# The spread of dt by DMA in a Mamba layer, begun three groups ahead of its scan instead of two

## The chip, the cores and the metric

The kernel runs on one core of a Trainium2 chip. The metric is the device time of one execution in microseconds, taken as the median of several executions. The engines are named as in the profile: PE is the matrix engine (PEld its loading of weights), DVE the vector engine, ACT the scalar engine with its function tables, POOL the GpSimd engine, and SP the engine whose sequencer, SPq, only issues transfers here.

## The reference, cut to what matters

Four layers follow each other on an image of 2 x 128 x 64 x 64 in float32. The change lies in the first of them, two Mamba blocks over sequences of 4096 tokens, each followed by a feed-forward block:

```python
xz = x @ in_w.T;  u, z = split(xz)
u = silu(causal_conv4(u) + conv_b)
dt, Bm, Cm = split(u @ xproj_w.T)             # 8, 16 and 16 wide
dt = softplus(dt @ dt_w.T + dt_b)             # 256 channels
dA = exp(dt[..., None] * A)                   # 256 channels x 16 states
dBu = (dt * u)[..., None] * Bm[:, :, None, :]
h = dA_t * h + dBu_t                          # for each token in turn
y = sum over states of h * C_t
y = (y + u * D) * silu(z) @ out_w.T
```

The three other layers (two self-attentions over 4096 positions and a multi-scale fusion) are not touched.

## The kernel before, in words

The first layer fills the time from about 60 us to 2190 us. Its work is cut into 32 items, one for each of two images, two blocks and eight chunks of 512 tokens. 256 channels times 16 states are 4096 recurrences, and 128 of them fit on the partitions at once, so an item has 32 scans of 128 x 512. Four scans (m = 0 to 3) share one pack of 32 channels and make a group: the 128 partitions hold the same 32 channels four times over, each time for another state. An item thus has 8 groups; below, "group 6" is the seventh group of an item and "slot 24" its first scan, out of slots 0 to 31.

What a group needs, with the names of the code:

- `dtb`, dt of the 32 channels laid four times over the partitions. `spread_dt(g)` (L325 to L329) does this by four transfers of 64 KB from the tile `dt`, on the SP queue. There are four buffers of it.
- `pdu`, dt times u spread in the same way, but by one matmul (`spread_dtu`, L334) into a PSUM buffer of which there is one. `times_b` (L340, DVE) multiplies it with `bb` into `h`, a tile of four 512-wide parts; five buffers serve `h`, and the hidden tile of the feed-forward block takes turns in them.
- `da`, the exponential of `dtb` times A (`decay`, L347, ACT), four PSUM buffers.
- the scan itself (L358, DVE). After the fourth scan of a group POOL saves the last column (L360) and multiplies `h` by `cb` (L361).
- `y_pair` (L373, PE), sixteen small matmuls that sum two groups over the states; `y_out` (L381, DVE) adds u times D once for each half of an item.

`bb` and `cb` are B and C of an item spread over the partitions. `spread_bc` (L297 to L305) does it once for each item: the tile `dbl`, which the projection `pd` (L291, PE) and a copy on ACT (L295) make, goes to DRAM as `dr`, and from there eight broadcast transfers of 256 KB each bring it back, four for `bb` and four for `cb`. These nine transfers are on the SP queue too.

The order of everything is written out by hand. A main loop goes over items and, within each, over 32 slots: in every slot it emits the spreads that are due, `y_pair`, one scan, the decay of four slots later, `times_b` of the next group, and then the background work of that slot from a list (`background`, L437 to L475): for the next item the convolution matmuls (L262), `xproj` (L291) in slot 13, `spread_bc` in slot 14, `soft_plus` (L315) in slot 17, `dt_end` (L321) in slot 18; for two layer normalisations at once the variance (L210) in slot 17, a Newton step in slots 20 and 21 (L226 on POOL, L227 on ACT, L231 on POOL), its spread over the partitions (`pr`, L235, PE) in slot 27; and the feed-forward block (L403, L415). Each engine runs its own instructions strictly in that order, and so does the queue of SP. An SP instruction whose data or buffer is not ready holds back all transfers behind it. The program also uses eight completion counters in turn for its transfers, so each transfer waits for the one issued eight before it.

Of the kernel before, what the change touches and what calls it, by code (L numbers as in the profile page):

```python
# [6 lines left out]
F32 = mybir.dt.float32  # L7
# [8 lines left out]
P = 128  # L16
CH = 512
# [50 lines left out]
def tile_conv_seq(ctx: ExitStack, tc, x, consts, vecs, wemb, wlay, wconv, wdt, wqkv, wsmall, wms, out):  # L68
# [39 lines left out]
    with ExitStack() as s, tc.manual_schedule():  # L108
        wp = s.enter_context(tc.tile_pool(name="l0w", bufs=1))
        sp = s.enter_context(tc.tile_pool(name="l0s", bufs=1))  # L110
# [23 lines left out]
        for l in range(NL):  # L134
            w = wp.tile([P, NWL - DI], F32, name=f"wl{l}")
# [30 lines left out]
        st = [{} for _ in items]  # L166
# [6 lines left out]
        def vl(name, i, k=0):  # L173
            return v1(f"{name}{items[i][1]}", k)
# [22 lines left out]

        def ln_square(w, k, i):
            if "sq" not in w:
                w["sq"] = sp.tile([P, 2, CH], F32, name="sq", tag="tmp", bufs=2)  # L200
                w["cen"] = sp.tile([P, 2, CH], F32, name="cen", tag="cen")
            pc = w.pop(("pc", k))
            nc.scalar.activation(w["sq"][:, k, :], pc, AF.Square)
            nc.scalar.copy(w["cen"][:, k, :], pc)
# [35 lines left out]

        def ln_shift(w, k, i, second):
            if second:
                dst = st[i]["x2"] = sp.tile([P, CH], F32, name="x2", tag="tmp", bufs=2)
            else:
                xn = st[i]["xn"] = sp.tile([P, KC - 1 + CH], F32, name="xn", tag="xn", bufs=2)
                if items[i][2] == 0:
                    nc.gpsimd.memset(xn[:, : KC - 1], 0.0)
                else:
                    nc.gpsimd.tensor_copy(xn[:, : KC - 1], prev_xn[0][:, CH : CH + KC - 1])
                prev_xn[0] = xn  # L250
                dst = xn[:, KC - 1 :]
            nc.scalar.activation(dst, w["cen"][:, k, :], AF.Identity, bias=vl("ln_b", i))  # L252
# [71 lines left out]
        def spread_dt(g):  # L324
            i, s_ = divmod(g, NST)  # L325
            o = st[i]["dtb", s_] = sp.tile([P, CH], F32, name="dtb", tag="dtb", bufs=4)
            k = 32 * (s_ % 4)
            for q in range(4):
                nc.sync.dma_start(o[32 * q : 32 * q + 32, :], st[i]["dt"][k : k + 32, s_ // 4, :])  # L329

        def spread_dtu(g):
            i, s_ = divmod(g, NST)
            pdu = st[i]["pdu", s_] = bc.tile([P, CH], F32, name="pdu", tag="bc")
            nc.tensor.matmul(pdu, lhsT=four(s_ % 4), rhs=st[i]["dtu"][:, s_ // 4, :], start=True, stop=True)  # L334

        def times_b(g):
            i, s_ = divmod(g, NST)
            h = st[i]["h", s_] = sp.tile([P, 4, CH], F32, name="h", tag="h", bufs=5)
            pdu = st[i].pop(("pdu", s_))
            nc.vector.tensor_tensor(h, st[i]["bc", 0], pdu.unsqueeze(1).to_broadcast([P, 4, CH]), ALU.mult)  # L340

        def decay(t):
            g, m = divmod(t, 4)
            i, s_ = divmod(g, NST)
            j, gg = divmod(s_, 4)
            da = st[i]["da", s_, m] = dap.tile([P, CH], F32, name="da", tag="da")
            nc.scalar.activation(da, st[i]["dtb", s_], AF.Exp, scale=am[items[i][1]][:, j, gg, m : m + 1])  # L347

        def scan(t):
            g, m = divmod(t, 4)  # L350
            i, s_ = divmod(g, NST)
            j, gg = divmod(s_, 4)
            b, l, c = items[i]
            if (b, l) not in carries:
                carries[b, l] = sp.tile([P, NJ, 4, 4], F32, name="carry", tag="carry", bufs=2)
                nc.gpsimd.memset(carries[b, l], 0.0)
            h, da = st[i]["h", s_], st[i].pop(("da", s_, m))
            nc.vector.tensor_tensor_scan(h[:, m, :], da, h[:, m, :], carries[b, l][:, j, gg, m : m + 1], ALU.mult, ALU.add)  # L358
            if m == 3:
                nc.gpsimd.tensor_copy(carries[b, l][:, j, gg, :].unsqueeze(2), h[:, :, CH - 1 : CH])  # L360
                nc.gpsimd.tensor_tensor(h, h, st[i]["bc", 1], ALU.mult)  # L361

        def y_pair(g):

            i, s_ = divmod(g, NST)
            j, gg = divmod(s_, 4)
            if gg == 0:
                st[i]["py", j] = yp.tile([P, CH], F32, name="py", tag="y")
            py = st[i]["py", j]
            for m in range(4):  # L370
                for k in range(2):
                    r = 32 * (gg + k)
                    nc.tensor.matmul(  # L373
                        py[r : r + 32, :], lhsT=sel, rhs=st[i]["h", s_ + k][:, m, :], start=(m == 0), stop=(m == 3),
                        tile_position=(0, r),
                    )
# [60 lines left out]
        def background(i):  # L437
# [28 lines left out]
            for k, (it, second) in enumerate(pair):  # L466
                at(12 + 2 * k, ln_centre, w, k, it)
                at(13 + 2 * k, ln_square, w, k, it)
                at(27, ln_spread, w, k, m), at(28, ln_scale, w, k, it)
                at(29, ln_shift, w, k, it, second)  # L470
# [13 lines left out]
        NG, NT = NI * NST, NI * NSL  # L484
        for i in range(-2, NI + 2):
            todo = background(i)
            for t_ in range(NSL):
                t = i * NSL + t_
                g, m = divmod(t, 4)
                if m == 0 and 0 <= g + 2 < NG:  # L490
                    spread_dt(g + 2)
                if m == 0 and 0 <= g + 1 < NG:
                    spread_dtu(g + 1)
                if m == 0 and g % 2 == 1 and 0 <= g - 3 < NG:
                    y_pair(g - 3)
                if 0 <= t < NT:
                    scan(t)
                if 0 <= t + 4 < NT:
                    decay(t + 4)
                if m == 3 and 0 <= g + 1 < NG:  # L500
                    times_b(g + 1)
                for f, a in todo[t_]:
                    f(*a)
# [14 lines left out]
    with ExitStack() as s, tc.manual_schedule():  # L518
        sp = s.enter_context(tc.tile_pool(name="ats", bufs=1))
# [9 lines left out]
        st = {}  # L529
# [158 lines left out]
        for now in range(NALL + LAG + 10):  # L688
            r, u = divmod(now, NU)
            w = now % 8  # L690
# [31 lines left out]
    with ExitStack() as s, tc.manual_schedule():  # L722
        sp = s.enter_context(tc.tile_pool(name="mss", bufs=1))
# [50 lines left out]
        for si in (2, 3):  # L774
            wgt[si] = sp.tile([P, SCALES[si]], F32, name=f"wgt{si}")
            for k in range(SCALES[si]):
                w = (k + 0.5) / SCALES[si] - 0.5
# [6 lines left out]
        st = [{} for _ in items]  # L784
# [386 lines left out]
```

## Time and profile before

| what | value |
|---|---|
| device time, median of 3 | 5351.36 us (5349.31 to 5352.06) |
| span of the profiled execution | 5360.6 us |
| busy over the span: PE, DVE, ACT, POOL | 91%, 71%, 43%, 43% |
| busy from 60 to 2250 us: PE, DVE, ACT, POOL | 1907.1, 1884.3, 1499.6, 1440.5 us of 2190 |
| granted PE clock from 60 to 2250 us, and after | 0.89 and 0.98 |
| mean time from one item to the next (items 1 to 30) | 65.19 us |
| `dtb` transfers | 1024 of 64 KB, median 2.0 us to landing |
| `bb`, `cb` transfers | 128 each of 256 KB, median 4.5 and 7.6 us to landing |

A group of the profile is all instructions of one line, engine and operation; its line gives the busy time and the mean of one, and after the bar how long the engine stood idle just before them, and what ended that. A wait is always put down to the event that came last. Lines of SPq are issues of transfers, and "to landing" is the time from the start of an issue to the transfer's completion.

### The profile page before, as it was taken

How to read it: one execution, taken by the hardware profiler on the slowest of the kernel's cores; microseconds unless marked ns; L12 is line 12 of the kernel's file. 1: busy time of each engine (PE TensorE's matmuls, PEld its weight loads, DVE VectorE, ACT ScalarE, POOL GpSimd, SP SyncE). 2: the span in 40 equal slices, each digit the busy share in tenths (PEclk: the TensorE clock that was granted, in tenths of full speed). 3: DMA queues.
4: the chain of work that ended last, by engine and by line, in shares of the span. 5: the costliest groups of instructions: out<-in, count | busy, mean ns of one | idle time of the engine just before them, and what ended most of it. 6: DMA issues, size and time to landing. Idle time of an engine off the chain costs nothing.

```text
span 5360.6 us, 48695 instructions
## 1 busy us (share of the span) xinstructions
PE 4900.6 (91%) x15085; PEld 2311.3 (43%) x15085; DVE 3798.2 (71%) x3810; ACT 2326.4 (43%) x2933; POOL 2287.5 (43%) x1948
## 2 busy tenths in 40 slices
PE   5888888888888898899999999999999998988997
PEld 1222222222222222356665566656666665333332
DVE  4998999889999999136663366667767775656665
ACT  4676777777777776212221122232323221223332
POOL 2766666666666767112221122223333332322221
PEclk8898889999898988899999999999999999999998
DMA  4222233222222232014442244444444442000000
GB/s 108 69 65 64 65 70 70 68 68 64 64 64 64 68 73 69 17 42 95 96 97 50 51 96 96 95 101 112 112 101 101 112 111 71 4 4 4 6 6 8
DMA packets 233843, 362.04 MB, mean 68 GB/s; under 512 B 87648, under 2 KB 88048, under 8 KB 225136
## 3 DMA queue, kind: packets, MB, share of 16 engines
q1 hardware_dynamic: 184432, 291.76, 23.2%
q10 hardware_dynamic: 49152, 67.17, 5.2%
q8 instruction: 121, 1.98, 0.2%
q14 instruction: 138, 1.13, 0.1%
HBM read 83.92 MB, written 6.29 MB: 17 GB/s over the span
## 4 chain that ended last, share of the span: by engine, by line
PE 59%; DVE 14%; DMA 10%; ACT 6%; SPq 4%; issue 4%; POOL 4%; ACTq 0%; DVEq 0%; POOLq 0%
PE pq L600 11%; PE po L647 11%; PE py L373 5%; PE pp L544 5%; DVE tr L627 4%; PE pu L262 4%; SPq L638 3%; DMA dtb<-dt 3%; DVE h L358 3%; DMA bb<-dr 3%; POOL h L361 3%; DMA pt<-tr 3%; PE pdu L334 2%; PE pf L861 2%; PE ph L403 2%
## 5 line engine op out<-in xcount | busy, mean ns | idle before, releaser
L634 POOL COPY pt<-tr 32x512 f32<-32x512 f32 x1024 | 628.0, 613 | 1680.7 <-DVE tr L627 911.8
L358 DVE TENSOR_TENSOR_SCAN h<-da,carry,h 128x512 f32<-128x512 f32 x1024 | 1240.2, 1267 | 97.6 <-ACT da L347 68.3
L361 POOL TENSOR_TENSOR h<-h,cb 128x2048 f32<-128x2048 f32 x256 | 1160.7, 4534 | 20.8 <-POOL carry L360 0.2
L604 DVE TENSOR_SCALAR_CACHE_REDUCE sc<-pq 128x1024 f32<-128x1024 f32 x512 | 625.9, 1223 | 760.6 <-PE pq L600 748.4
L647 PE MATMUL po<-pt,vt 128*128 128x256 f32 x4096 | 968.1, 380 | 4.8 <-DMA pt<-tr 4.8
L600 PE MATMUL pq<-k,q 128*128 128x512 f32 x2048 | 962.1, 592 | 4.8 <-ACT q L532 3.4
L647 PEld LDWEIGHTS po<-pt,vt 128*128 128x128 f32 x4096 | 776.4, 190 | 265.4 <-issue 170.6
L347 ACT ACTIVATE da<-dtb,am 128x512 f32<-128x512 f32 x1024 | 686.8, 685 | 390.3 <-DVE h L358 250.2
L613 ACT ACTIVATE sc<-sc,nm 128x4096 f32<-128x4096 f32 x128 | 474.8, 3709 | 721.9 <-DVE nm L611 615.6
L627 DVE STREAM_TRANSPOSE tr<-sc 128x2048 f32<-128x2048 f32 x256 | 589.3, 2302 | 37.9 <-DMA pt<-tr 24.5
L340 DVE TENSOR_TENSOR h<-bb,pdu 128x2048 f32<-128x2048 f32 x256 | 580.0, 2266 | 25.0 <-POOL carry L360 15.4
L373 PE MATMUL py<-h,sel 128*32 128x512 f32 x2048 | 506.7, 638 | 1.7 <-POOL h L361 1.7
L600 PEld LDWEIGHTS pq<-k,q 128*128 128x128 f32 x2048 | 383.5, 190 | 277.8 <-issue 248.7
L334 PE MATMUL pdu<-dtu,fsel 128*128 128x512 f32 x512 | 327.4, 726 | 87.8 <-DVE h L340 87.6
L532 ACT ACTIVATE q<-pqq,vec 128x256 f32<-128x256 f32 x64 | 30.4, 474 | 606.6 <-PE pqq L544 361.2
L373 PEld LDWEIGHTS py<-h,sel 128*32 128x32 f32 x2048 | 114.5, 117 | 412.5 <-issue 406.8
L544 PE MATMUL pp<-xt,wq 128*128 128x512 f32 x576 | 251.8, 598 | 6.6 <-DMA wq<-in_wqkv 6.2
L262 PE MATMUL pu<-xn,wu 128*128 128x512 f32 x512 | 246.1, 614 | 2.7 <-ACT xn L252 1.7
L235 PE MATMUL pr<-rs,kc 2*128 2x512 f32 (+1 forms) x128 | 117.1, 1059 | 133.1 <-POOL rs L231 126.9
L334 PEld LDWEIGHTS pdu<-dtu,fsel 128*128 128x128 f32 x512 | 95.2, 214 | 303.5 <-DVE h L340 187.9
L888 PE MATMUL pqkv<-f,ws 128*128 128x512 f32 x384 | 197.8, 641 | 10.2 <-ACT q L895 6.3
L950 DVE TENSOR_TENSOR ov<-v,pw 128x2048 f32<-128x2048 f32 x64 | 146.2, 2284 | 63.4 <-PE pw L943 63.3
(191 smaller groups left out, 5089.1 us busy)
## 6 DMA issues: line engine op xcount, KB each, us to landing
pt<-tr SPq DMA_DIRECT2D x2048, 64.0 KB, 2.0
dtb<-dt SPq DMA_DIRECT2D x1024, 64.0 KB, 2.0
pt<-tr ACTq DMA_DIRECT2D x1024, 64.0 KB, 2.1
bb<-dr SPq DMA_DIRECT2D x128, 256.0 KB, 4.5
cb<-dr SPq DMA_DIRECT2D x128, 256.0 KB, 7.6
xt<-in_x SPq DMA_DIRECT2D x16, 256.0 KB, 5.1
xr<-in_x SPq DMA_DIRECT2D x16, 256.0 KB, 3.1
out<-ot SPq DMA_DIRECT2D x16, 256.0 KB, 2.0
```

What stands on the lines that cost most here:

```text
L334: nc.tensor.matmul(pdu, lhsT=four(s_ % 4), rhs=st[i]["dtu"][:, s_ // 4, :], start=True, stop=True)
L340: nc.vector.tensor_tensor(h, st[i]["bc", 0], pdu.unsqueeze(1).to_broadcast([P, 4, CH]), ALU.mult)
L347: nc.scalar.activation(da, st[i]["dtb", s_], AF.Exp, scale=am[items[i][1]][:, j, gg, m : m + 1])
L358: nc.vector.tensor_tensor_scan(h[:, m, :], da, h[:, m, :], carries[b, l][:, j, gg, m : m + 1], ALU.mult, ALU.add)
L361: nc.gpsimd.tensor_tensor(h, h, st[i]["bc", 1], ALU.mult)
L373: nc.tensor.matmul(py[r : r + 32, :], lhsT=sel, rhs=st[i]["h", s_ + k][:, m, :], start=(m == 0), stop=(m == 3), tile_position=(0, r),)
L544: nc.tensor.matmul(ps, lhsT=wq[:, which, tap, :], rhs=rhs, start=(tap == 0), stop=(tap == 8))
L600: nc.tensor.matmul(pq[:, i, :], lhsT=st["q", r, grp][:, it * P : (it + 1) * P], rhs=st["k"][:, at : at + CH], start=True, stop=True)
L604: nc.vector.tensor_scalar(dst, pq, 1.0, None, ALU.mult, ALU.max, accum_out=st["mx"][:, c2 : c2 + 1])
L627: nc.vector.transpose(tr, half.rearrange("p (t r f) -> p r t f", r=NB, f=32))
L634: nc.gpsimd.tensor_copy(dst, src)
L647: nc.tensor.matmul(st["po", r, grp], lhsT=st["vt"][:, jt, :], rhs=rhs, start=(jt == 0), stop=(jt == N // P - 1))
```

## The change

`spread_dt` is called three groups ahead of the scan instead of two. The number of `dtb` buffers stays at four. Beside this, two tiles of the layer normalisation, `sq` and `x2`, which shared two buffers, get one of their own each. The purpose is to have the spread dt on hand earlier than the exponentials ask for it.

```diff
         def ln_square(w, k, i):
             if "sq" not in w:
-                w["sq"] = sp.tile([P, 2, CH], F32, name="sq", tag="tmp", bufs=2)
+                w["sq"] = sp.tile([P, 2, CH], F32, name="sq", tag="sq")
...
             if second:
-                dst = st[i]["x2"] = sp.tile([P, CH], F32, name="x2", tag="tmp", bufs=2)
+                dst = st[i]["x2"] = sp.tile([P, CH], F32, name="x2", tag="x2")
...
                 g, m = divmod(t, 4)
-                if m == 0 and 0 <= g + 2 < NG:
-                    spread_dt(g + 2)
+                if m == 0 and 0 <= g + 3 < NG:
+                    spread_dt(g + 3)
                 if m == 0 and 0 <= g + 1 < NG:
                     spread_dtu(g + 1)
```

In the emitted program this moves the four transfers of `dtb` for group 6 of every item from just behind the item's nine transfers `dr`, `bb` and `cb` to just ahead of them; the order of all other transfers of that queue relative to these stays, but for the small loads `xr`, which now stand behind one more group of `dtb`. The order on PE, DVE, ACT and POOL is the same as before.

## The prediction

> **What bounds the kernel now.** I read the waits of DVE first, because in the first layer PE (1907 of 2190 us) and DVE (1884 us) are both nearly full and DVE carries the scans. From 60 to 2250 us, who DVE waited for:
>
> ```profile
> DVE u L381 <- PE py L373: 84.9, 51, 8.6
> DVE h L358 <- ACT da L347: 68.3, 40, 3.8
> ```
>
> The scans waited 68.3 us for an exponential, in 40 places. The same view of ACT and of the SP queue:
>
> ```profile
> ACT da L347 <- DVE h L358: 250.2, 216, 2.9
> ACT da L347 <- DMA dtb<-dt: 133.9, 31, 6.1
> ```
> ```profile
> SPq L300 <- ACT dbl L295: 767.0, 32, 38.2
> SPq L329 <- ACT da L347: 374.2, 95, 9.2
> ...
> SPq L329 <- DMA cb<-dr: 93.3, 128, 2.1
> SPq L329 <- DMA bb<-dr: 56.6, 90, 1.3
> ```
>
> ACT waits for a spread `dtb` once in each item, 4.3 us on average. SPq waits 24 us per item (767.0/32) for `dbl` before it can issue `dr`, and afterwards 128 `dtb` issues, four in each item, wait for the landing of a `cb`: that is the wait for the transfer eight before. So I went through one item by the timeline, item 14. The queue:
>
> ```profile
> 1026.60 0.31 SPq L300 DMA_DIRECT2D dr<-dbl  x1
> 1028.25 1.70 SPq L305 DMA_DIRECT2D bb<-dr  x4
> 1030.05 1.76 SPq L305 DMA_DIRECT2D cb<-dr  x4
> 1031.85 30.59 SPq L329 DMA_DIRECT2D dtb<-dt  x28
> ```
>
> The last `dtb` before this `dr` was issued at 1001.3 us, and then the queue stood for 24.7 us. The first four `dtb` behind `cb` are group 6. Read in narrow windows, the first lands 8.5 us after its issue at 1031.85, the fourth 5.9 us after 1035.22, at 1041.2; an undisturbed one takes 2.0. ACT and DVE at that time:
>
> ```profile
> 1037.50 0.63 ACT L221 ACTIVATE nt<-rs 2x512 f32<-2x512 f32 x1
> 1041.28 0.69 ACT L347 ACTIVATE da<-dtb,am 128x512 f32<-128x512 f32 x1 [3.14 <-DMA dtb<-dt]
> 1041.90 0.70 ACT L227 ACTIVATE nt<-nt,c 2x512 f32<-2x512 f32 x1
> ```
> ```profile
> 1039.66 0.74 DVE L381 SCALAR_TENSOR_TENSOR u<-u,vec,py 128x512 f32<-128x512 f32 x1
> 1042.00 4.85 DVE L358 TENSOR_TENSOR_SCAN h<-da,carry,h 128x512 f32<-128x512 f32 x4 [1.59 <-ACT da L347]
> ```
>
> The scan of slot 24 could have begun at 1040.41 and begins at 1042.00, straight after its exponential. Is this on the path that sets the end? The chain of waits around it:
>
> ```profile
> 1029.53 5.67 DMA bb<-dr
> 1035.20 0.02 issue
> 1035.22 5.95 DMA dtb<-dt
> ...
> 1041.28 0.70 ACT da L347
> 1041.97 0.03 issue
> 1042.00 2.47 DVE h L358 x2
> ```
>
> It passes through it, and then `times_b` and the `pdu` matmul at 1049.08, which waits for `times_b` to empty the one PSUM buffer.
>
> **What the Trainium skill says.** "DMA: Bandwidth & Descriptors", section "Anatomy of one DMA", says that a wait is served at the issuing sequencer before dispatch, not in the transfer engines: a blocked `dr` therefore blocks `dtb` behind it. The trace agrees (24.7 us). The same page, "Queues, rings and completion order", says that each engine takes the descriptors of a ring in order: a `dtb` behind 2 MB of broadcasts waits for these. The trace agrees (8.5 against 2.0 us). "TensorE: Matmul & The Clock Gate", Part 1, says that PE runs at half clock after an idle window of some 3.4 us and is released after a busy one. The trace agrees: the clock in the stretch 1376 to 1380 of item 19 is 0.50, and `pdu` there takes 2.07 us for its two passes instead of the 0.86 of full clock. No page is needed for prices; the trace has all operations.
>
> **The change part by part.**
>
> *sq and x2.* With a shared pair of buffers in strict turn (one `sq`, one `x2` per item from the second item on) each already has its own. The emitted waits on ACT, PE, DVE and POOL keep their kind and number. Cost 0.
>
> *Group 6 of `dtb` ahead of `dr`.* No transfer is added. With four buffers it must wait until group 2 is read out; of its exponentials, emitted in slots 4 to 7, the last ends at 1009.6 us in item 14. Four issues of 0.6 us and 2.0 us to landing put it on hand at about 1014, 24 us before ACT reaches it (1038.1). The new wait stands ahead of `dr`, which cannot go before 1026.6 anyway: 14 us of slack from 1012. So `dr`, `bb` and `cb` keep their times. `xr` now stands behind one more group, which went at 999.45 to 1001.3; `xr` lands in 3.1 us, and its matmul comes at 1017.7. Cost 0.
>
> *Group 7 takes the place behind `cb`.* Its four transfers land as group 6 did, at about 1041.2. Its first exponential stands four places further on: exponentials of slots 24 to 27 and L227 come first (below, until 1042.9). No stall in this item. Where ACT does stop, by up to 2 us, DVE has the four scans of group 6 (4.8 us) and `times_b` (2.3) to do first.
>
> *What DVE gains.* Without the stall ACT issues slot 24 at 1038.14, done at 1038.83, and DVE scans at 1040.41, gaining 1.59. But the next exponential stands behind L227, which needs the Newton product of POOL, L226, which ends at 1040.32. So L227 can start at 1040.36, and the exponential of slot 25 is done 0.62 + 0.72 us later at 1041.70, against 1041.61 when DVE is ready. Gain of slot 25 onward: 1.51 us.
>
> The same arithmetic over items 0 to 30: the waits before the scan of slot 24 sum to 63.0 us (0.88 to 3.80 each; the other 5.3 of the 68.3 stand before slot 23 and belong to the softplus tables). L226 ends, relative to DVE ready, between 1.0 us before and 1.1 us after. Where it is late (items 3, 10, 12, 15, 17 at 1.0 to 1.1, some at 0.5) the scan of slot 25 waits for L227 and about that much is lost, 10.8 us in all. Net 63.0 - 10.8 = **52.2 us**, 1.68 per item.
>
> *Does it reach the end?* The loop closes as follows. `pdu` of the next item's first group starts when `times_b` of group 7 ends; from there PE works without a gap for 21.4 to 23.0 us to the `py` that `y_out` waits for (1.98 us of DVE idle per item); from `y_out` DVE works almost without a gap to slot 24, and to `times_b` of group 7 again. The wait of slot 24 is the one large hole of that second part. Everything in the next item hangs on `pdu` through PE, so it moves as a whole. The softplus and Newton chain on ACT and POOL also starts from PE's `pd`, so its place relative to DVE stays, and the 52.2 us recur. After the layer nothing changes. Sum: 5351.4 - 52.2 = **5299 us**.
>
> **The rivals.**
>
> *R1, PE's clock goes against it.* PE is already at half clock when `pdu` starts. In items 18 to 29 the period is near 64.9 us and PE's part takes 21.9 us on average, with the cold spell ending 3.5 us after `pdu` starts (item 19); a loop shortened by 1.7 us meets the clock's changes at other places, and the worst item before took 23.0. One us more in each item takes 31 us: 5330. For it: the clock changes in the trace in steps of 3.41 us. Against: items 1 to 17, with varied places, average only 0.35 us more.
>
> *R2, the clock helps.* PE's idle time before `pr` (L235 waits for POOL's L231, which waits for L227) shrinks from 3.65 to about 1.8 us. If PE then stays at full clock, `pdu` and the first `py` lose up to 1.2 and 1.1 us; the DVE wait of 1.98 before `y_out` can absorb it as gain. About 1.1 per item more, 34 us: 5265. Against it: `pr` is the only work between two `pdu` 7 us apart, so PE remains over half idle there.
>
> *R3, one wait replaces the other.* Group 7 stalls ACT as long as group 6 did, and DVE with it: 0 gained, 5351. Speaks against it that the ring of four `da` and L227 stand before it.
>
> *R4, slower.* If the buffer of group 6 came free later than `dbl`, `dr` and `bb` would be late and `times_b` of the next item's first group with them; or the clock costs over 1.7 us in each item. Half a microsecond more than the gain in each item gives 5367. The 14 us of slack speak against the first, the worst item of before (0.9 us over the mean of 22.1) against the second.
>
> **How the numbers follow.** The main case gets 0.62 (5299, with 0.3 us per item either way 5290 to 5309), R1 0.14, R2 0.14, R3 0.06, R4 0.04. R1 and R2 set the ends, with a few us beyond each: 5256 to 5334, which leaves out R3, R4 and a part of R1 and R2, 0.19 together. Faster by over 0.2% (10.7 us) is the main case, R2 and nearly all of R1: 0.89. Within 0.2%: R3 with a rest of R1, 0.06. Slower 0.05.
>
> **What would show it.** In the new profile ACT's wait for `dtb` falls from 133.9 to some 10 to 50 us (the prologue's 6.1 stays, group 7 may stop ACT briefly); DVE's wait for ACT falls from 68.3 to under 20; SPq's wait for `dbl` falls from 24 to some 14 us per item; the period goes from 65.2 to about 63.5. PE's mean clock in the layer (0.89) tells R1 from R2. The prediction fails if DVE's wait turns up elsewhere in the item, at L381 or L340.

## The result and the profile after

The changed kernel takes 5332.93 us (median of 6, 5328.56 to 5338.58) against 5351.23 us for the kernel before: ratio 0.9966, 95% interval 0.9953 to 0.9979. It is faster by 18 us, where 52 were predicted; the range of 5256 to 5334 just holds it.

The stall that the change was made for is gone. Who DVE, ACT and the SP queue waited for from 60 to 2250 us, in the kernel after (total us, times, longest):

```profile
DVE u L381 <- PE py L373: 91.5, 57, 8.6
...
DVE h L340 <- issue: 28.5, 21, 1.7
DVE h L358 <- ACT da L347: 21.5, 28, 1.2
DVE h L340 <- POOL carry L360: 7.7, 9, 1.2
```
```profile
ACT da L347 <- DVE h L358: 265.6, 255, 2.9
...
ACT hid L404 <- PE ph L403: 73.6, 68, 2.5
ACT nt L227 <- POOL nt L226: 64.3, 34, 2.8
...
ACT ve L214 <- PE var L210: 25.5, 26, 1.1
...
ACT da L347 <- DMA dtb<-dt: 6.0, 2, 5.3
```
```profile
SPq L329 <- ACT da L347: 656.2, 142, 9.8
SPq L300 <- ACT dbl L295: 454.0, 32, 37.0
SPq L329 <- DMA cb<-dr: 92.4, 128, 2.1
```

ACT's wait for `dtb` fell from 133.9 to 6.0 us, nearly all of it the prologue. `dr` is still held for its data, but the queue now spends ten of those 24 us per item on the buffer of group 6, as foreseen (454.0/32 = 14.2). The scans' wait for ACT fell from 68.3 to 21.5 us. But other waits of DVE grew: `times_b` (L340) behind "issue", which is PE's `py` of groups 4 and 5 holding the buffer of `h` that the next item's first group needs (5.3 us before, 28.5 now), and `y_out` (L381) behind `py` (84.9 to 91.5). ACT waits for PE's `var` 25.5 us instead of 9.5, and the scan of slot 23 waits for ACT behind it. The lines of the kernel before for two of these:

```profile
DVE h L340 <- issue: 5.3, 5, 1.7
```
```profile
ACT ve L214 <- PE var L210: 9.5, 12, 1.1
```

The idle time of DVE per item, at the places where it changed, read from the timeline between the first scans of items 1 and 30:

| DVE idle, us per item | before | after |
|---|---|---|
| before the scan of slot 24 (the stall) | 1.95 | 0.00 |
| before `times_b` of the next item's first group | 0.68 | 1.21 |
| before the scan of slot 23 | 0.18 | 0.64 |
| before `y_out` of slot 23 | 0.47 | 0.68 |
| before the scan of slot 25 | 0.00 | 0.11 |
| time from item to item | 65.19 | 64.54 |

1.95 us were taken away and 1.31 came back in the same item. All of what came back, but for the 0.11 us before slot 25, waits for PE, directly or through ACT. Item 12 of the kernel after, PE's timeline (start, length, instructions):

```profile
887.42 3.57 PE L210 MATMUL var<-sq,kc 128*2 128x512 f32 x4 [1.29 <-ACT dt L315]
890.92 2.04 PE L334 MATMUL pdu<-dtu,fsel 128*128 128x512 f32 x2
892.89 3.63 PE L373 MATMUL py<-h,sel 128*32 128x512 f32 x16
896.45 1.12 PE L334 MATMUL pdu<-dtu,fsel 128*128 128x512 f32 x2
898.49 2.69 PE L235 MATMUL pr<-rs,kc 2*128 2x512 f32 x4 [0.91 <-POOL rs L231]
904.29 2.07 PE L334 MATMUL pdu<-dtu,fsel 128*128 128x512 f32 x2 [3.12 <-DVE h L340]
906.30 5.38 PE L373 MATMUL py<-h,sel 128*32 128x512 f32 x16
```

The `pdu` at 904.29 belongs to the next item's first group. It takes 2.07 us, where the one at 896.45, at full clock, takes 1.12. The `py` behind it takes 5.38 us, where the one at 892.89 takes 3.63. The same place in item 9 of the kernel before:

```profile
718.12 3.77 PE L235 MATMUL pr<-rs,kc 2*128 2x512 f32 x4 [2.69 <-POOL rs L231]
723.21 2.07 PE L334 MATMUL pdu<-dtu,fsel 128*128 128x512 f32 x2 [1.32 <-DVE h L340]
725.21 4.80 PE L373 MATMUL py<-h,sel 128*32 128x512 f32 x16
```

There was a spell of half clock here before the change too, but it ended 4.4 us after this `pdu` began; now it ends 5.6 us after. `var` is at half clock as well, and this became more frequent: 102 of the 128 `var` matmuls start in such a stretch, 47 before. The granted clock in stretches of item 12 of the kernel after (the third number from the end, ahead of the DMA share):

```profile
888.00:892.00 4.00, 4.00 (x6) 0.76 (x4) 3.31 (x3) 2.90 (x4) 3.90 (x3) 0.50 1.05 221
...
900.00:904.00 4.00, 1.18 (x2) 0.00 (x0) 4.00 (x3) 1.82 (x3) 3.92 (x3) 0.50 0.41 100
904.00:908.00 4.00, 3.71 (x6) 0.87 (x8) 3.90 (x5) 0.69 (x1) 4.00 (x2) 0.50 0.26 66
908.00:912.00 4.00, 4.00 (x15) 1.08 (x12) 2.47 (x3) 2.52 (x4) 1.40 (x3) 0.77 0.00 0
```

I take as PE's clock loss half the summed length of the stretches granted at 0.5 that begin before 2180 us: 228.7 us before, 264.5 after. The 35.8 us more are close to the 34 us that are missing in the result, but not every us of half clock stands on the path that sets the end, so the nearness of the two numbers proves nothing by itself.

Around `pr`, from slot 24 on, the half-clock time did not grow: 10.2 us per item before and 9.7 after (means of items 2 to 30, by the trace's record of the clock). It only lies later relative to the work. `pr` waits less than before, but PE's rest moved from ahead of it to behind it (3.60 and 1.45 us before, 1.24 and 2.91 after). All 187 changes of the clock in the trace of the kernel after lie on one grid of 3.413 us, within 0.01 us, and the 171 of the trace before on one too. So a `pdu` that starts earlier within a step does not end the spell sooner. The clock rises 4.28 us after the start of the next item's first `pdu` on average before, 5.34 after, and from this `pdu` to the `py` that `y_out` waits for, PE takes 22.1 us on average before and 22.6 after. Around `var`, up to slot 24, the half-clock time did grow, from 3.1 to 5.7 us per item.

In 15 of the 31 items after, the time from item to item lies within 0.1 us of 64.85, which is 19 steps of 3.413. In 19 of the items 2 to 30 the clock rises 5.4 to 5.7 us after the `pdu`, in one before; an item that falls out of this place is followed, within a few items, by some that are back in it.

### The profile page after: what moved, and what is told of

Its sections match the earlier page's. It is cut to its first block, busy times and chain, and to the rows that moved or that the text cites. A ratio compares the mean times of both kernels' runs of the same rounds, so it can differ in the third digit from the quotient of the medians.

```text
span 5331.3 us, 48726 instructions
## 1 busy us (share of the span) xinstructions
PE 4908.7 (92%) x15085; PEld 2306.1 (43%) x15085; DVE 3796.5 (71%) x3810; ACT 2326.8 (44%) x2933; POOL 2286.9 (43%) x1948
## 3 DMA queue, kind: packets, MB, share of 16 engines
q14 instruction: 138, 1.13, 0.1%
## 4 chain that ended last, share of the span: by engine, by line
PE 58%; DVE 13%; POOL 12%; issue 7%; DMA 3%; ACT 3%; SPq 3%; ACTq 0%; DVEq 0%; POOLq 0%
PE pq L600 12%; PE po L647 12%; POOL h L361 9%; PE py L373 5%; PE pp L544 5%; DVE tr L627 4%; PE pu L262 3%; SPq L638 3%; PE pf L861 2%; DVE h L358 2%; DMA pt<-tr 2%; PE pdu L334 2%; PE ph L403 2%; PE pqkv L888 2%; PE pqq L544 2%
## 5 line engine op out<-in xcount | busy, mean ns | idle before, releaser
L358 DVE TENSOR_TENSOR_SCAN h<-da,carry,h 128x512 f32<-128x512 f32 x1024 | 1241.1, 1265 | 52.0 <-ACT da L347 21.5
L340 DVE TENSOR_TENSOR h<-bb,pdu 128x2048 f32<-128x2048 f32 x256 | 579.5, 2264 | 41.1 <-issue 28.5
L373 PE MATMUL py<-h,sel 128*32 128x512 f32 x2048 | 521.1, 654 | 0.5 <-POOL h L361 0.5
L888 PE MATMUL pqkv<-f,ws 128*128 128x512 f32 x384 | 197.4, 640 | 10.2 <-ACT q L895 6.3
L360 POOL COPY carry<-h 128x4 f32<-128x4 f32 x256 | 47.6, 186 | 317.4 <-DVE h L358 313.7
```

The lines of the kernel that those rows point to most:

```text
L373: nc.tensor.matmul(py[r : r + 32, :], lhsT=sel, rhs=st[i]["h", s_ + k][:, m, :], start=(m == 0), stop=(m == 3), tile_position=(0, r),)
```

## The experiments

Theory C (clock): the removed stall was a real saving of some 52 us, and PE's half clock took most of it back. Rival N (Newton chain): with `dtb` out of the way the product on POOL (L226) and L227 hold the exponentials, ACT's new wait of 64.3 us. Rival D: DVE's own work sets the loop. None of these kernels leaves out a part of the computation. The kernel before was timed again beside each group of experiments, with medians from 5351 to 5356 us; ratios are to the one timed beside, and a few us between runs of different groups carry no weight.

**1. The earlier spread alone.** `sq` and `x2` go back to their shared pair of buffers.

```diff
-w["sq"] = sp.tile(..., name="sq", tag="sq")
+w["sq"] = sp.tile(..., name="sq", tag="tmp", bufs=2)
...
-dst = st[i]["x2"] = sp.tile(..., name="x2", tag="x2")
+dst = st[i]["x2"] = sp.tile(..., name="x2", tag="tmp", bufs=2)
```

> The changed kernel with sq and x2 put back on their shared pair of buffers, so only the earlier spread of dt is left. Every theory here expects the time of the changed kernel, about 5333 us: each of the two tiles already had a buffer to itself from the second item on. If the separate buffers did part of the work, it lands between 5333 and 5351.

5332.15 us, ratio 0.9964 (0.9950 to 0.9978). The separate buffers do nothing that can be seen; the change is the order of the queue.

**2. Repeated matmuls in PE's rests, after and before.** The same PSUM tile is written again with the same values: seven matmuls more in an item, fourteen instructions of PE.

```diff
+for _ in range(4 if s_ == 7 else 1):        # spread_dtu
     nc.tensor.matmul(pdu, ...)
...
+for _ in range((2, 3)[k]):                  # ln_spread
     nc.tensor.matmul(w["pr", k], ...)
...
+for _ in range(2 if j == 1 else 1):         # dtproj
     nc.tensor.matmul(st[i]["pt", j], ...)
```

> The changed kernel with idle stretches of PE filled by repeating matmuls into the PSUM tile that they have just written (pdu of group 7 four times, pr two and three times, the second pt twice), 15 to 20 matmuls more in an item, none of them on work that another engine waits for at once. Clock theory (PE's half clock takes back the gain): PE stays at full clock around slots 24 to 31, the pdu of the next item falls from 2.08 to 0.86 us and the first py from 5.4 to 3.6, and the time falls by 2 to 3 us in each item, to 5235 to 5275. Newton-chain theory (after the change POOL's and ACT's Newton product holds the scans): no gain, 5333 to 5345, since PE only has more to do.

> The kernel before with the same repeated matmuls. Clock theory: here too PE's half-clock time falls, and the time goes to 5275 to 5315; and with the clock out of the way the earlier spread is worth close to the 52 us that were predicted, so this run stands 40 to 60 us above after_full_clock. Newton-chain theory: the two stay 18 us apart, as without the repeats.

5348.70 us (ratio 0.9994, 0.9985 to 1.0002) and 5404.42 us (1.0101, 1.0088 to 1.0115). Both are slower than their originals, and both lie outside the times expected by theory C; the first is outside those of rival N too. The two are 56 us apart, which is in theory C's 40 to 60 and not rival N's 18, but this supports theory C little, because the repeats cost time of their own: the longer `pr` holds up the `pdu` behind it, which starts 1.46 us after `times_b` releases it in the kernel before and 1.12 us in the kernel after, where it was 0.05 us without repeats. The clock was not held either, and why not is the most instructive line of this study. PE in the kernel after with repeats (line numbers are shifted by up to three), and the granted clock:

```profile
1035.89 3.70 PE L337 MATMUL pdu<-dtu,fsel 128*128 128x512 f32 x8 [0.16 <-DVE h L343]
1039.52 4.55 PE L236 MATMUL pr<-rs,kc 2*128 2x512 f32 x10
1044.01 1.32 PE L337 MATMUL pdu<-dtu,fsel 128*128 128x512 f32 x2
1045.26 5.08 PE L376 MATMUL py<-h,sel 128*32 128x512 f32 x16
```
```profile
1036.00:1040.00 4.00, 4.00 (x9) 1.62 (x10) 3.87 (x4) 3.44 (x6) 3.09 (x4) 1.00 0.44 106
1040.00:1044.00 4.00, 4.00 (x10) 1.48 (x8) 3.90 (x4) 1.69 (x3) 3.92 (x3) 1.00 0.42 103
1044.00:1048.00 4.00, 4.00 (x11) 1.03 (x12) 4.00 (x5) 1.08 (x2) 4.00 (x1) 0.60 0.27 66
```

PE is busy for all of these 12 us and still falls to half clock at 1044.8 us, after 4.5 us of `pr`, whose operands have 2 rows. So either the clock does not follow PE's busy time, or a matmul on a corner of the array counts as rest. The clock loss was 187.7 us, still most of the 264.5, and 203.1 us in the kernel before with repeats.

**3. DVE delayed.** One copy ahead of the scan of slot 24.

```diff
+if t_ == 24 and 0 <= t < NT:
+    nc.vector.tensor_copy(scr, kc[:, :512])
 if 0 <= t < NT:
     scan(t)
```

> The changed kernel with one copy of 128 x 512 on DVE into an unused tile ahead of the scan of slot 24 in each item, 0.3 to 0.7 us of DVE time. Clock theory: the loop of most items is held at 64.85 us, nineteen of the clock's steps of 3.41 us, and DVE has slack; the time rises by under 6 us. If DVE's own work sets the loop, it rises by the copy's full length in 32 items, 10 to 22 us.

5347.95 us (ratio 0.9988, 0.9982 to 0.9995), 15 us more than the changed kernel. The copies took more than I had assumed, 35.0 us in all:

```profile
L498 DVE COPY scr<-kc 128x512 f32<-128x512 f32 x32 | 35.0, 1093 | 0.0
```

Four tenths of them reached the end. That misses the under 6 us of theory C, and it lies in the 10 to 22 us of rival D only because the copies were longer: rival D asked for their full length, which was 35. DVE's waits show where the rest went (the kernel after has 7.7, 21.5 and 28.5 us in these lines):

```profile
DVE h L340 <- POOL carry L360: 17.6, 22, 1.3
DVE h L358 <- ACT da L347: 13.6, 20, 1.0
DVE h L340 <- issue: 11.3, 8, 1.6
```

All waits of this view together fell from 212 to 193 us. Per item, the idle time before `times_b` of the next item's first group fell from 1.21 to 0.96 us, before slot 23 from 0.64 to 0.46, before `y_out` from 0.68 to 0.55 and before slot 25 from 0.11 to nothing, and the clock loss fell to 247.5 us. So the waits that came back with the change shrink again when DVE comes later: the loop has slack for DVE, but not for all of the copy.

**4. The array's share alone.** No matmul is added; `var` gets 128 columns instead of 2, and `pr` 128 rows instead of 2, of which all but two are zero.

```diff
-    nc.tensor.matmul(var[:n], lhsT=kc[:, at : at + n], ...)
+    nc.tensor.matmul(var, lhsT=kc[:, at : at + P], ...)
...
-    nc.tensor.matmul(w["pr", k], lhsT=pick(k, n), rhs=w["rs"][:n], ...)
+    nc.tensor.matmul(w["pr", k], lhsT=pick(k, P), rhs=w["rs"], ...)   # rs: 128 rows
```

> The changed kernel in which two kinds of matmul use the whole array, with no matmul added: var gets weights 128 columns wide instead of 2 (the further rows of its result are not read), and pr gets 128 rows instead of 2 (the tile of factors is zero below the first two). In the runs with repeated pr matmuls PE was busy without a gap and its clock still fell to half in the middle of them. Theory A (the clock follows how much of the array works, so matmuls of 2 rows or 2 columns count as rest): PE loses less time to half clock than the 264.5 us of the changed kernel, and the time falls to 5290 to 5325. Theory B (only PE's idle time counts): no change, 5328 to 5340.

5340.49 us (ratio 0.9973, 0.9961 to 0.9985): no gain in time, outside theory A's range and at the edge of theory B's. The clock loss fell to 221.9 us, so the wide matmuls do something to the clock. All of that is around `pr`, where the half-clock time fell from 9.7 to 6.2 us per item; around `var` it went from 5.7 to 6.4, and DVE's wait before slot 23 grew from 0.64 to 0.97 us. The gaps around them remain.

**5. Full matmuls in the gaps, after and before.** On top of 4, six matmuls of 128 x 128 x 512 in each item, into PSUM tiles that are overwritten later: one ahead of the second `pt`, three in slot 24 behind `pdu`, two in slot 27 behind `pr`.

```diff
+def full(i, n):                   # slots 24 and 27, into the bank of the next py
+    for _ in range(n):
+        nc.tensor.matmul(st[i]["py", 1], lhsT=cm, rhs=kc[:, :CH], start=True, stop=True)
...
```

> The same, and in PE's idle stretches six full 128 x 128 x 512 matmuls in each item, into PSUM tiles that a later matmul overwrites (one ahead of the second pt, three behind pdu of group 7, two behind pr). Clock theory: PE stays at full clock from slot 15 to the next item's slot 4, the pdu of the next item takes 0.86 us and the first py 3.6, and the time falls to 5220 to 5275. If the clock is not what takes the gain back: 5330 to 5360.

> The kernel before with the same wide matmuls and the same six matmuls in each item. Clock theory: 5265 to 5320, and 40 to 65 us above after_fill, which is the gain that was predicted for a clock that stays as it is. If something other than the clock takes the gain back, the distance stays near the 18 us between the two kernels themselves.

5271.08 us (ratio 0.9846, 0.9829 to 0.9862) and 5326.61 us (0.9950, 0.9935 to 0.9964): the first inside the range of theory C, the second 7 us above it, and **55.5 us apart**. The clock losses are 34.1 and 41.0 us. PE in the kernel after with the six matmuls:

```profile
996.18 1.13 PE L336 MATMUL pdu<-dtu,fsel 128*128 128x512 f32 x2 [0.87 <-DVE h L342]
997.15 2.74 PE L385 MATMUL py<-kc 128*128 128x512 f32 x6
999.99 1.98 PE L235 MATMUL pr<-rs,kc 128*128 128x512 f32 x4
1001.81 1.88 PE L385 MATMUL py<-kc 128*128 128x512 f32 x4
1005.07 1.13 PE L336 MATMUL pdu<-dtu,fsel 128*128 128x512 f32 x2 [1.38 <-DVE h L342]
1006.13 3.63 PE L375 MATMUL py<-h,sel 128*32 128x512 f32 x16
```

The `pdu` of the next item and the `py` behind it come at full clock, 1.13 and 3.63 us. DVE's waits, first after, then before with the six matmuls:

```profile
DVE u L389 <- PE py L375: 56.7, 32, 8.6
...
DVE h L360 <- ACT da L349: 32.0, 31, 1.2
```
```profile
DVE h L360 <- ACT da L349: 83.5, 31, 4.5
DVE u L389 <- PE py L375: 61.9, 33, 10.3
```

The wait for `py` at the item's change has vanished from `times_b` in both. So has DVE's wait before slot 23. Between the two, the scans' wait for ACT differs by 51.5 us, and the time by 55.5: with the clock held, the removed stall is worth what it measures. The stall is not the same size as in the kernel before, though. With `var` at full clock DVE comes to slot 24 earlier and waits there 2.68 us per item instead of 1.95, about 23 us in the layer, which more than covers the 7 us above its range.

**6. The six matmuls without the wide var and pr.** The diff of 5 on the changed kernel without that of 4.

> The changed kernel with the six full matmuls in each item, but var and pr as they were, with 2 columns and 2 rows. Clock theory, in the form that small matmuls count as rest for the clock: less of the gain than in after_fill, 5285 to 5320, with PE's loss to half clock between 34 and 268 us. In the form that only gaps count: the same as after_fill, 5265 to 5277.

5276.80 us (ratio 0.9850, 0.9835 to 0.9864), clock loss 63.1 us. By the time, the gaps are what matters, in the range for that form of theory C and outside the other; the interval overlaps that of after_fill, so the widening is worth a few us at most when the gaps are filled.

**7. The later Newton step, without and with the filled gaps.** The POOL product stays in slot 20; the ACT instruction and the second POOL product go behind the exponential of slot 26.

```diff
-at(20, ln_newton, w, m), at(21, ln_step, w, m)
+at(20, ln_newton, w, m), at(22, ln_half, w, m), at(22, ln_step, w, m)
```

> The changed kernel with the second half of the Newton step (one ACT instruction and one of POOL) put two slots later, so that the exponentials of slots 25 and 26 stand ahead of it on ACT. Newton-chain theory (it took back the gain): 5300 to 5318. Clock theory: the scans no longer wait there, but PE's part still ends where its clock rises, so within 8 us of the changed kernel, 5325 to 5341.

> The kernel after_fill with the same later Newton step. There, at full clock, the scan of slot 25 is the largest remaining wait of DVE, 1.04 us in each item. Clock theory: now that wait does count, and removing it gives 20 to 35 us, 5236 to 5252. Otherwise 5265 to 5277.

Without filled gaps 5329.55 us (ratio 0.9951, 0.9934 to 0.9968), within the range of theory C and outside that of rival N; the interval overlaps that of the changed kernel. This fits the table above, in which DVE waited only 0.11 us per item before slot 25: ACT's 64.3 us for the product cost DVE little. With filled gaps 5242.19 us (ratio 0.9782, 0.9767 to 0.9796), 29 us below after_fill, in the range of theory C. The same edit is worth a few us at most or 29, depending on whether the gaps are filled. This last kernel beats all others here: 2.2% below the kernel before, with an item every 61.3 us.

**8. The repeats of 2, with wide var and pr.** Number and place of the matmuls as in after_full_clock.

> after_full_clock (pdu of group 7 four times, pr two and three times, the second pt twice) with var 128 columns wide and pr 128 rows high; the matmuls are the same in number, place and length. Theory A (matmuls that use 2 rows or 2 columns of the array count as rest for the clock): PE's loss to half clock falls from the 187.7 us of after_full_clock to under 80, the first pdu and py of an item come at full clock, and the time falls from 5349 to 5265 to 5300. Theory B (only gaps count): 5335 to 5355, as after_full_clock.

5278.23 us (ratio 0.9853, 0.9837 to 0.9870) against 5348.70, and a clock loss of 90.5 against 187.7 us. That is theory A's range of times, though its clock loss was expected under 80. The `pdu` of the next item and the `py` behind it came at full clock in each of the items 2 to 30, as theory A expected:

```profile
1014.61 1.12 PE L337 MATMUL pdu<-dtu,fsel 128*128 128x512 f32 x2
1015.66 3.63 PE L376 MATMUL py<-h,sel 128*32 128x512 f32 x16
```

The half-clock time around `pr` fell from 6.5 us per item to nothing. Around `var` it is 3.8 us in both kernels. By its place, the gain belongs to the rows of `pr`: repeats with 2 rows did not hold the clock, the same repeats with 128 rows, nearly all zeros, do. For the columns of `var` no effect is seen.

## Why the prediction was wrong

*The change part by part* held. The separate buffers of `sq` and `x2` cost and bring nothing (5332.15 against 5332.93 us). The `dtb` of group 6 arrives in time: item 14's four go at 996.2 to 999.7 us in the run after, and `dr` at 1013.1 still goes straight behind the copy of `dbl`. Group 7 hardly stalls ACT: outside the prologue, at most 0.7 us of ACT's waits for `dtb` are left. The gain on DVE at slot 24 is 1.95 us per item, all of it.

*What DVE gains, 52.2 us,* held in its kind: with the clock held, 55.5 us between the two kernels with filled gaps. That the sizes agree so well is partly luck. The stall was larger there (2.68 us per item instead of 1.95), and the subtraction of 10.8 us for L227, about 0.35 us per item, was too small there: the scan of slot 25 waits 1.04. The two errors nearly cancel. Without filled gaps the subtraction was too large: the scan of slot 25 waits 0.11 us per item, probably because the wait before slot 23 now gives POOL time.

*"Does it reach the end?"* failed. The step said that PE works for 21.4 to 23.0 us from `pdu` and that everything hanging on it moves as a whole. It took PE's durations as fixed. They depend on the clock, whose stretches do not move with the loop: 1.31 of the 1.95 us came back, 1.20 of them as waits on `py` and `var`, 64.54 us per item instead of 63.5, and 5333 us instead of 5299. The dependence stood in the trace of the kernel before: PE's part took 21.7 us in an item where the clock rose 3.5 us after `pdu` began, and 23.1 where it rose 6.3 us after. The sign that the prediction named for its failure, DVE's wait turning up at L381 or L340, is what came, and PE's mean clock in the layer, named to tell R1 from R2, went from 0.89 to 0.88.

This is the rival R1, which stood at 0.14 with 5330 us. Its mechanism was right and its time near; the argument against it was wrong. I compared PE's part in items of different position (0.35 us) and forgot the second place with half clock, ahead of `var`, where the longer spell costs DVE 0.46 us before slot 23 and 0.21 before `y_out`. That R1's 5330 us came within 3 us is in part luck too, since it counted one place and not both. R2, that a shorter rest before `pr` would hold the full clock, did not come: the rest before `pr` shrank even more than it said, to 1.24 us, and reappeared behind `pr`, and the half clock stayed. The Trainium skill, "TensorE: Matmul & The Clock Gate", Part 1, told of the half clock after a rest; I used it to explain durations and not to ask what the loop's length would do to them.

What stays open: why the clock falls more often at `var` in the kernel after, and whether the many items of 64.85 us are truly locked to the clock's step. For the lock speak the grid and the return to one place; twice in a row, two neighbouring items of the delayed kernel also take 64.17 and 65.53 us, together 38 steps. That many items are alike is no sign by itself, because in after_fill many take 62.07 or so, which is no multiple of the step. No run tests it alone.

## What to carry to other kernels

When two engines hand work to each other and one of them has a clock that falls in its rests, a wait removed elsewhere can come back as slower matmuls: look at the granted clock on both sides of the rest before counting the gain. Filling PE's rests with full-size matmuls into a tile that is overwritten later was worth 56 us on the changed kernel (5333 to 5277), and 62 with the wide `var` and `pr` (5271), about three times the change itself, and made the next edit count at its full size. Fill with matmuls that use all rows of the array: repeats with 2 rows made the kernel slower.

## What the runs showed of the hardware that was not expected

PE fell to half clock at 1044.8 us while busy without a gap since 1035.9, in a run of matmuls with 2 rows. The skill's Part 1, named above, says that the clock follows how busy PE has been; in these runs busy time alone doesn't decide, and the idle window of some 3.4 us that the prediction took from it is not needed. With the same `pr` matmuls on 128 rows, the half-clock time around them fell from 6.5 us per item to nothing, and the time by 70 us (5348.70 to 5278.23). And in item 12 of the kernel after, PE falls to half clock at 899.6 us, within `pr`, with a rest of only 0.91 us ahead of it.
